# Graph layer in one kernel: edge features in one transfer, 512-column products, and another order where layers meet

## The chip, the cores and the metric

The kernel runs on one core of a Trainium2 chip. The metric is the device time in microseconds (us) of one launch. TensorE multiplies and transposes, VectorE (DVE in the profile) and ScalarE (ACT) do elementwise work, GpSimd (POOL) issues the gathers, and SyncE (SP) issues nearly all other transfers.

## The reference

A graph with 3125 nodes of 256 features and 100,000 edges sorted by destination, all in float32. Cut to what matters:

```python
xn = layernorm(x)
# graph part: one message per edge, summed per destination
m   = concat([xn[src], edge_attr_3])                  # 256 + 3 features
h_N = segment_sum(relu(m @ W1.T + b1), dst)
gnn = l2_normalize(relu(concat([xn, h_N]) @ W2.T))
# mixer part: four layers over all nodes
h = xn
for l in range(4):
    a = layernorm(h)
    q = softmax over each head's 32 features of (a @ Wq) * scale
    k = softmax over all nodes of (a @ Wk) * scale
    h = h + (q @ (k.T @ v)) @ Wo + bo                 # v = a @ Wv
    h = h + gelu(layernorm(h) @ W1 + b1) @ W2 + b2
x = x + gnn + h
# sixteen experts, two per node, with weights from a gate
return x + layernorm(y + moe(y)),  y = layernorm(x)
```

## The kernel before, in words

Nodes stand as 25 tiles of 125, grouped in seven blocks: five of four tiles, one of three and one of two. The activations stay in on-chip memory (`xm`). The mixer is written as stages over one block: `stage_k` and `stage_q` (products with Wk, Wq and their softmax steps), `stage_ek` and `stage_qT` (transposes of the results), `stage_m` (the running sum of k and a), `context` (L508: from the finished sum to one matrix `mo`, a chain of four short products with VectorE or ScalarE between them), `stage_y`, `stage_ln2`, `stage_t2`, `stage_f1`, `stage_f2` (the feed-forward part), and `stage_stats`, `stage_ln1`, `stage_t1` (layer norm for the next layer). The order of calls from L655 to L734 is written out by hand and is the order of TensorE, ScalarE and GpSimd; VectorE and SyncE are put in order by the framework's scheduler, at build time.

The edge part runs beside the layers. By linearity, `xn @ W1h` is computed once (`stage_proj`) and stored in memory. Edges are cut into 784 chunks of 128, eight chunks to a group, 98 groups. For each chunk GpSimd gathers 128 rows (L255, `load_chunk`). A group is split in four strips of two chunks; a strip has one of four row groups of TensorE.

- `message_step` (L284): the product of the three edge features (and a one, for the bias) with their weights, `pw` (L294), one product of 256 columns for each chunk; VectorE adds it to the gathered rows (L298), ScalarE applies relu (L299), VectorE makes the one-hot matrix `hot` (L301).
- `sum_step` (L265): products with `hot` sum a group's messages into 32 destinations per strip (`pq`, L279); the sum of two groups ago is transposed (`win_ps`, L270) and added to `hNT` (L273).

A planner spreads these steps. Each has a due place in groups (`due`, L308): gathers 1.25 groups ahead, messages at half, sums at whole numbers. Each stage reports its TensorE columns by `worked`, which advances `place` and runs the steps that have come due; so they enter the order between two stages' instructions. A gather that comes due waits for a one-element copy (`tick`, L334) of the stage's result, so that GpSimd isn't ahead of the stage. The calls `worked(12 * D)` stand where TensorE would have nothing else; in the last layer, `stage_g` (products of the graph update) takes these places.

What is left of the plan is flushed at L730. Then all engines read a flag (L802) and take or skip a branch (`any_order`, for inputs whose destinations lie far apart; skipped here). The memory of the edge phase is then given to the pool `gates`.

Of the kernel before, what the change touches and what calls it, by code (L numbers as in the profile page):

```python
# [17 lines left out]
D = 256  # L18
P = 128
# [45 lines left out]
def gps_layer(ctx: ExitStack, tc: tile.TileContext, a, out):  # L65
# [60 lines left out]
    with ExitStack() as ph:  # L126
# [9 lines left out]
        def mm_tile(name):  # L136
            return psum.tile([P, 512], F32, tag="mm", name=name)
# [37 lines left out]
        w1w = edge.tile([P, D], F32, name="w1w", bufs=1)  # L175
# [25 lines left out]
        for s in range(S):  # L201
            nc.sync.dma_start(w1w[s * W:s * W + 4, :], a["gnn_W1w"])
# [40 lines left out]
        def load_chunk(c):  # L243

            g, j = divmod(c, G)
            if j == 0:
                ea = edge.tile([P, SC * P], F32, name="ea")
                for s in range(S):
                    e0 = (g * S + s) * SC * P
                    nc.sync.dma_start(ea[s * W:s * W + 4, :], a["eaT"][:, e0:e0 + SC * P])  # L250
                groups_[g] = [], ea
            gats = groups_[g][0]
            if j % (G // 2) == 0:
                gats.append(edge.tile([P, 2, SC, D], F32, name="gat", bufs=6))
            nc.gpsimd.indirect_dma_start(  # L255
                out=gats[-1][:, (j // SC) % 2, j % SC, :], out_offset=None, in_=proj,
                in_offset=bass.IndirectOffsetOnAxis(ap=src_i[:, c:c + 1], axis=0))
# [26 lines left out]
        def message_step(g):  # L284
            if g % 2 == 0:
                bases.extend(nc.values_load_multi_w_load_instructions(
                    base_i[:, g * S:min((g + 2) * S, NS)], engines=[mybir.EngineType.DVE],
                    min_val=0, max_val=N - 1,
                    skip_runtime_bounds_check_because="a dst is a node")[1])
            gats, ea = groups_[g]  # L290
            pws = [mm_tile("pw").rearrange("p (i d) -> p i d", i=SC) for _ in range(S)]
            for i in range(SC):
                for s in range(S):
                    nc.tensor.matmul(pws[s][:, i, :], ea[s * W:s * W + 4, i * P:(i + 1) * P],  # L294
                                     w1w[s * W:s * W + 4, :], start=True, stop=True)
            for s in range(S):
                msg = gats[s // 2][:, s % 2]
                nc.vector.tensor_add(msg, msg, pws[s])  # L298
                nc.scalar.activation(msg, msg, AF.Relu)  # L299
# [105 lines left out]
        def stage_stats(b):  # L405
            for t in BLOCKS[b]:
                stats(tmp, xm[:, t, :], t)
# [100 lines left out]
        def context(l):  # L508
# [8 lines left out]
            worked(12 * D)  # L517
# [6 lines left out]
            worked(12 * D)  # L524
# [128 lines left out]
        with tc.manual_schedule(engines=in_order):  # L653

            prepared = windows()  # L655
            stage_xn(0)
            stage_xh1(0)
            stage_xnT(0)
# [3 lines left out]
            for b in range(NB + 1):  # L662
                if b < NB:
                    stage_k(0, b)
                    if b + 2 < NB:
                        stage_xn(b + 2)
                    stage_q(0, b)
                if b > 1:
                    next(prepared, None)
                if b > 0:  # L670
                    stage_m(0, b - 1)
                if b + 1 < NB:
                    stage_xh1(b + 1)
                    stage_xnT(b + 1)
# [4 lines left out]
                if b < NB:  # L679
                    if b > 1:  # L680
                        next(prepared, None)
                    stage_ek(0, b)
                    stage_qT(0, b)
                if b == NB - 2:
                    for _ in prepared:
                        pass
                    spread = True
            for l in range(last):
                start_layer(l)
                context(l)  # L690
                load(l + 1, "Wk", "Wq", "Wv")
                stage_y(l, 0)
                stage_ln2(0)
                stage_y(l, 1)
                worked(12 * D)
                stage_t2(l, 0)
                worked(12 * D)
                for b in range(NB):
# [13 lines left out]
                    stage_stats(b)  # L712
                    if b > 0:
                        stage_k(l + 1, b - 1)
# [4 lines left out]
                    stage_ln1(b)  # L719
                stage_ek(l + 1, NB - 2)  # L720
                stage_qT(l + 1, NB - 2)
# [11 lines left out]
            stage_qT(last, NB - 1)  # L733
            stage_m(last, NB - 1)  # L734

        def any_order():
# [13 lines left out]
            def chunk(e0, n):  # L750
# [33 lines left out]
                nc.tensor.matmul(pw[:n, 0, :], ea[:4, :n], w1w[:4], start=True, stop=True)  # L784
# [26 lines left out]
        w2n = wts.tile([P, KC, D], F32, tag="wq", name="w2n")  # L811
# [120 lines left out]
        with tc.manual_schedule(engines=in_order - {mybir.EngineType.Pool}):  # L932
# [3 lines left out]
            parts = [(0, slice(0, 1)), (0, slice(1, 2)), (1, slice(0, 1))]  # L936

            def worked(columns, mark=None):
                if columns == 12 * D and parts:
                    stage_g(*parts.pop(0))  # L940

            context(last)
            stage_y(last, 0)
            stage_ln2(0)
# [267 lines left out]
def device_arrays(inputs):  # L1212
# [16 lines left out]
    d = {"x": i["x"], "eaT": np.pad(eaT, ((0, 0), (0, fill))), "src": i["src"], "dst": i["dst"]}  # L1229
    d["src_c"], d["dst_c"] = chunked(i["src"]), chunked(i["dst"])  # L1230
    w1 = i["L0_gnn_W1"]
    d["gnn_W1h"], d["gnn_W1w"] = w1[:, :D].T, np.concatenate([w1[:, D:].T, i["L0_gnn_b1"][None]])
# [33 lines left out]
```

## Time and profile before

| | us |
|---|---|
| median of 3 runs (1987.17 to 1989.06) | 1988.45 |
| the profiled execution's own time | 1994.73 |
| its span, first to last instruction | 1993.0 |
| TensorE busy | 1807.7 |
| VectorE, ScalarE, GpSimd busy | 1165.1, 743.6, 1126.5 |
| gathers, L255, 784 of them | 761.9 |
| `pw`, L294, 1568 records (two passes for each product) | 114.6 |

How to read it: a matmul of float32 shows as two records, one for each pass; a transpose shows as one. The busy time of a group of matmuls is the union of its records, since they overlap. The granted clock (PEclk) is the share of TensorE's full speed that it was given. The layers' boundaries lie at about 135, 530, 950 and 1350 us; the experts run from about 1690 to 1918 us.

### The profile page before, as it was taken

Reading aid. Unit: us, or ns where it says so; the run is one execution under the profiler, and the core shown is the slowest. Engines: PE = TensorE matmul, PEld = TensorE weight load, DVE = VectorE, ACT = ScalarE, POOL = GpSimd, SP = SyncE. Lnnn points to the kernel's source line nnn. Section 1 sums busy time; section 2 is a strip of 40 time slices with the busy share of each in tenths; the row PEclk is TensorE's granted clock in tenths of the full one; section 3 lists DMA queues with packets and bytes.
Section 4 is the critical chain, followed back from the end, with each engine's and each line's share of the span. In section 5 each row is a group of like instructions: output and inputs, shape, how many; then the busy total and the mean of one; then the engine's idle time right before and its main releaser. Section 6 shows DMA issues by size and latency. Waiting matters only on the chain. (4 is left out here: it accounts for less than half of the span.)

```text
span 1993.0 us, 30766 instructions
## 1 busy us (share of the span) xinstructions
PE 1807.7 (91%) x9749; PEld 1269.3 (64%) x9749; DVE 1165.1 (58%) x3761; ACT 743.6 (37%) x1343; POOL 1126.5 (57%) x1429
## 2 busy tenths in 40 slices
PE   6988999999888999999889999998999994999963
PEld 4764656666655666667546666666777783888841
DVE  7654566666664666766656666765646653333326
ACT  3543444344533444544333444443222231222202
POOL 1026777677667777777677777771114435545512
PEclk9998999999988999999889999999999996999987
DMA  6123333233433233334423233333211113777744
GB/s 188 66 77 92 89 85 88 79 88 93 129 98 91 84 93 91 89 84 127 118 81 89 85 90 87 89 89 100 67 29 29 28 19 116 241 259 260 273 130 120
DMA packets 83294, 210.74 MB, mean 106 GB/s; under 512 B 26523, under 2 KB 42306, under 8 KB 78389
## 3 DMA queue, kind: packets, MB, share of 16 engines
q0 software_dynamic: 44800, 118.16, 20.6%
q1 hardware_dynamic: 37246, 87.31, 13.9%
q10 hardware_dynamic: 1078, 3.20, 0.6%
q8 instruction: 84, 1.38, 0.3%
q14 instruction: 86, 0.70, 0.1%
HBM read 187.34 MB, written 21.19 MB: 105 GB/s over the span
## 5 line engine op out<-in xcount | busy, mean ns | idle before, releaser
L255 POOL DMA_INDIRECT gat<-proj,src_i x784 | 761.9, 972 | 212.4 <-issue 163.4
L581 PE MATMUL f_ps<-h2T,ww 128*128 128x500 f32 (+2 forms) x896 | 360.6, 551 | 6.4 <-ACT h2T L339 5.8
L299 ACT ACTIVATE gat<-gat 128x512 f32<-128x512 f32 x392 | 237.6, 630 | 341.0 <-DVE gat L298 315.4
L591 PE MATMUL f_ps<-ww,gT 128*125 128x256 f32 x1600 | 362.3, 382 | 0.0
L298 DVE TENSOR_TENSOR gat<-gat,pw 128x512 f32<-128x512 f32 x392 | 245.5, 680 | 162.1 <-PE pw L294 138.3
L591 PEld LDWEIGHTS f_ps<-ww,gT 128*125 128x125 f32 x1600 | 295.1, 188 | 58.4 <-issue 10.5
L581 PEld LDWEIGHTS f_ps<-h2T,ww 128*128 128x128 f32 x896 | 167.0, 192 | 168.5 <-issue 122.8
L583 ACT ACTIVATE gT<-f_ps,ffb 128x500 f32<-128x500 f32 (+2 forms) x224 | 135.6, 631 | 136.4 <-PE f_ps L581 135.8
L279 PE MATMUL pq<-gat,hot 128*32 128x256 f32 x1568 | 137.6, 405 | 22.4 <-ACT gat L299 22.3
L273 DVE TENSOR_TENSOR hNT<-hNT,win_ps 128x64 f32 x392 | 84.7, 216 | 74.4 <-PE win_ps L270 64.4
L925 POOL DMA_INDIRECT slots<-rec,at x50 | 59.5, 1189 | 110.0 <-DVE rs_u L113 63.7
L596 DVE TENSOR_TENSOR xm<-xm,f_ps 125x512 f32<-125x512 f32 (+1 forms) x52 | 34.7, 667 | 138.7 <-PE f_ps L591 136.4
L1120 PE MATMUL e_ps<-ew,hs 128*128 128x256 f32 x464 | 112.8, 381 | 2.2 <-DVE o L1124 2.2
L294 PE MATMUL pw<-w1w,ea 4*128 4x256 f32 x1568 | 114.6, 403 | 0.0
L1127 POOL DMA_INDIRECT outs<-o,ids x58 | 57.4, 989 | 100.6 <-DVE o L1125 97.5
L458 PE MATMUL q_ps<-wwq,hT 128*125 128x256 f32 x400 | 99.8, 402 | 4.6 <-DVE gat L298 3.6
L563 POOL TENSOR_TENSOR xm<-xm,b 125x1024 f32<-125x1024 f32 (+2 forms) x28 | 59.9, 2140 | 77.6 <-DVE xh L122 58.5
L547 PE MATMUL y_ps<-mo,qT 128*125 128x256 f32 x400 | 98.0, 397 | 4.9 <-DVE mo L538 4.9
L294 PEld LDWEIGHTS pw<-w1w,ea 4*128 4x128 f32 x1568 | 72.5, 185 | 45.0 <-issue 34.5
L495 PE MATMUL m_ps<-xh,ek 125*128 125x257 f32 x400 | 97.9, 398 | 1.8 <-ACT ek L481 1.8
L279 PEld LDWEIGHTS pq<-gat,hot 128*32 128x32 f32 x1568 | 49.6, 112 | 77.9 <-ACT gat L299 45.3
L1120 PEld LDWEIGHTS e_ps<-ew,hs 128*128 128x128 f32 x464 | 85.2, 190 | 20.4 <-issue 4.5
(222 smaller groups left out, 2652.8 us busy)
## 6 DMA issues: line engine op xcount, KB each, us to landing
ew<-ffn_w SPq DMA_DIRECT2D x37, 1154.0 KB
gat<-proj,src_i POOLq DMA_INDIRECT x784
ww<-mix_W SPq DMA_DIRECT2D x8, 1024.0 KB
ea<-eaT SPq DMA_DIRECT2D x392, 4.0 KB
ogs<-outs SPq DMA_DIRECT2D x6, 448.0 KB
ogs<-outs ACTq DMA_DIRECT2D x6, 448.0 KB
out<-ogs SPq DMA_DIRECT2D x6, 448.0 KB
xnT_d<-stage SPq DMA_DIRECT2D x5, 500.0 KB
```

Source lines behind the costliest of these rows:

```text
L255: nc.gpsimd.indirect_dma_start(out=gats[-1][:, (j // SC) % 2, j % SC, :], out_offset=None, in_=proj, in_offset=bass.IndirectOffsetOnAxis(a ...
L279: nc.tensor.matmul(pq[s * W:(s + 1) * W, :], hot[:, s * SC + i, :], gats[s // 2][:, s % 2, i, :], start=(i == 0), stop=(i == SC - 1))
L294: nc.tensor.matmul(pws[s][:, i, :], ea[s * W:s * W + 4, i * P:(i + 1) * P], w1w[s * W:s * W + 4, :], start=True, stop=True)
L298: nc.vector.tensor_add(msg, msg, pws[s])
L299: nc.scalar.activation(msg, msg, AF.Relu)
L458: nc.tensor.matmul(ps[:, i, :], hT[:, c, cols(o + i)], wt["Wq"][:, c, :], start=(c == 0), stop=(c == KC - 1))
L495: nc.tensor.matmul(ps, st["ek", b][:, i, c * P:(c + 1) * P], xh1s[b % 2][:, i, :], start=(i == 0), stop=(i == n - 1))
L547: nc.tensor.matmul(ps[:, i, :], qT[:, c, cols(t0 + i)], mo[:, c, :], start=(c == 0), stop=(c == KC - 1))
L581: nc.tensor.matmul(ps, wt["W1"][:, c, f * P:(f + 1) * P], st["h2T", b][:, c, :m], start=(c == 0), stop=(c == KC - 1))
L583: nc.scalar.activation(gT[:, f, :m], ps, AF.Gelu, bias=ffb[:, l, f:f + 1])
L591: nc.tensor.matmul(ps[:, i, :], st["gT", b][:, f, cols(o + i)], wt["W2"][:, f, :], start=(f == 0), stop=(f == NF - 1))
L1120: nc.tensor.matmul(ps[:, j, :], x["hs"][:, f, j * P:(j + 1) * P], x["w2"][:, f, :], start=(f == 0), stop=(f == NEF - 1))
```

## The change

- Edge features: they are laid out on the host as one block of 128 x 128 numbers for each group, each strip's two chunks in eight rows, the rest zero. One transfer for a group takes the place of four.
- Products: the weights are laid out as eight rows of 512 columns, block-diagonal, so that one product of eight rows gives both chunks of a strip side by side. There are four products for a group instead of eight.
- Start: `stage_xnT` goes ahead of `stage_xh1`.
- Changes of layer: the planner is held (`held`) from the last block's statistics to `stage_y` of block 0 of the next layer; at fixed places in between, `fill(2)` runs up to one message and `fill(1)` up to one sum, with the gathers that stand ahead of them and no `tick`. The last block's layer norm goes ahead of `stage_k` of the block before. The last block's `stage_q` moves into `context`, its `stage_qT` behind `stage_y` of block 1. The columns of the held part are taken out of `total`, which makes the plan's rate higher elsewhere.
- End: in the last layer's `context` the places are taken by `stage_q` and three parts of `stage_g`; `w2n` no longer takes the place of Wq, which is still in use, and lies in `gates`.

```diff
-                ea = edge.tile([P, SC * P], F32, name="ea")
-                for s in range(S):
-                    e0 = (g * S + s) * SC * P
-                    nc.sync.dma_start(ea[s * W:s * W + 4, :], a["eaT"][:, e0:e0 + SC * P])
+                ea = edge.tile([P, P], F32, name="ea")
+                nc.sync.dma_start(ea, a["ea_g"][g])
...
-            pws = [mm_tile("pw").rearrange("p (i d) -> p i d", i=SC) for _ in range(S)]
-            for i in range(SC):
-                for s in range(S):
-                    nc.tensor.matmul(pws[s][:, i, :], ea[s * W:s * W + 4, i * P:(i + 1) * P],
-                                     w1w[s * W:s * W + 4, :], start=True, stop=True)
+            pws = [mm_tile("pw") for _ in range(S)]
+            for s in range(S):
+                nc.tensor.matmul(pws[s], ea[s * W:s * W + SC * 4, :], w1w[s * W:s * W + SC * 4, :],
+                                 start=True, stop=True)
+            pws = [pw.rearrange("p (i d) -> p i d", i=SC) for pw in pws]
...
-        total = (DEPTH - 1) * (attention + forward + 60 * D)
+        at_end = sum(len(r) * (2 * KC * TP + KC * D + 2 * KC * P + KC * (D + 1)) for r in BLOCKS[-2:])
+        total = (DEPTH - 1) * (attention + forward) - (DEPTH - 1) * (at_end + BT * KC * D)
...
-            if not spread:
+            if not spread or held:
                 return
...
+        def fill(kind):
+
+            while due and due[-1][1] in (0, kind):
+                _, k, step, i = due.pop()
+                step(i)
+                if k == kind:
+                    return
...
-            worked(12 * D)
+            between[0]()
             ps = mm_tile("meanT_ps").rearrange("p (h m) -> p h m", h=KC)
...
-            worked(12 * D)
+            between[1]()
             ps = mm_tile("ctx_ps")[:, :D].rearrange("p (c m) -> p c m", c=KC)
...
-            worked(12 * D)
+            between[2]()
             ps = mm_tile("mo_ps").rearrange("p (c d) -> p c d", c=KC)
...
+            between[3]()
...
+            stage_xnT(0)
             stage_xh1(0)
-            stage_xnT(0)
...
-                context(l)
+                more = (lambda kind: None) if l == 0 else fill
+                context(l, [lambda: stage_q(l, NB - 1), lambda: more(1), lambda: None, lambda: more(2)])
                 load(l + 1, "Wk", "Wq", "Wv")
                 stage_y(l, 0)
+                held = False
                 stage_ln2(0)
                 stage_y(l, 1)
-                worked(12 * D)
+                stage_qT(l, NB - 1)
                 stage_t2(l, 0)
-                worked(12 * D)
...
                     stage_stats(b)
+                    if b == NB - 1:
+                        stage_ln1(b)
+                        held = True
+                        fill(2)
                     if b > 0:
                         stage_k(l + 1, b - 1)
...
                 stage_ek(l + 1, NB - 2)
-                stage_qT(l + 1, NB - 2)
                 stage_t1(l + 1, NB - 1)
                 stage_m(l + 1, NB - 2)
                 stage_k(l + 1, NB - 1)
-                stage_q(l + 1, NB - 1)
+                stage_qT(l + 1, NB - 2)
                 stage_ek(l + 1, NB - 1)
-                if l + 1 < last:
-                    stage_qT(l + 1, NB - 1)
-                    stage_m(l + 1, NB - 1)
+                fill(1)
+                stage_m(l + 1, NB - 1)
...
-        w2n = wts.tile([P, KC, D], F32, tag="wq", name="w2n")
+        w2n = gates.tile([P, KC, D], F32, name="w2n")
...
-            parts = [(0, slice(0, 1)), (0, slice(1, 2)), (1, slice(0, 1))]
...
-            context(last)
+            context(last, [lambda: stage_q(last, NB - 1), lambda: stage_g(0, slice(0, 1)),
+                           lambda: stage_g(0, slice(1, 2)), lambda: stage_g(1, slice(0, 1))])
             stage_y(last, 0)
+            stage_qT(last, NB - 1)
```

More of the change, by code (lines that the diff above doesn't have):

```diff
@@ L174, in gps_layer @@
         w1h = wts.tile([P, KC, D], F32, tag="wo", name="w1h")
-        w1w = edge.tile([P, D], F32, name="w1w", bufs=1)
+        w1w = edge.tile([P, SC * D], F32, name="w1w", bufs=1)
         proj = dram.tile([N, D], F32, name="proj")
@@ L201, in gps_layer @@
         for s in range(S):
-            nc.sync.dma_start(w1w[s * W:s * W + 4, :], a["gnn_W1w"])
+            nc.sync.dma_start(w1w[s * W:s * W + SC * 4, :], a["gnn_W1w"])
         nc.sync.dma_start(ffb, a["mix_b1"])
@@ L503, in stage_m, with context @@
             worked(n * KC * (D + 1), msum[:1, 0, :1])
-        def context(l):
+        def context(l, between):
             nonlocal mo
@@ L661, in gps_layer @@
             stage_t1(0, 0)
[L662 to L666, printed above, removed]
+            for b in range(NB):
+                stage_k(0, b)
+                if b + 2 < NB:
+                    stage_xn(b + 2)
+                if b < NB - 1:
                     stage_q(0, b)
+                else:
+                    held = True
                 if b > 1:
@@ L672, in gps_layer @@
                 if b + 1 < NB:
+                    stage_xnT(b + 1)
                     stage_xh1(b + 1)
-                    stage_xnT(b + 1)
                     if b > 1:
@@ L678, in gps_layer @@
                     stage_t1(0, b + 1)
[L679 to L682, printed above, removed]
+                if b > 1:
+                    next(prepared, None)
+                stage_ek(0, b)
+                if b < NB - 1:
                     stage_qT(0, b)
@@ L687, in gps_layer @@
                     spread = True
+            stage_m(0, NB - 1)
             for l in range(last):
                 start_layer(l)
-                context(l)
+                more = (lambda kind: None) if l == 0 else fill
+                context(l, [lambda: stage_q(l, NB - 1), lambda: more(1), lambda: None, lambda: more(2)])
                 load(l + 1, "Wk", "Wq", "Wv")
                 stage_y(l, 0)
+                held = False
                 stage_ln2(0)
                 stage_y(l, 1)
-                worked(12 * D)
+                stage_qT(l, NB - 1)
                 stage_t2(l, 0)
-                worked(12 * D)
                 for b in range(NB):
@@ L712, in gps_layer @@
                     stage_stats(b)
+                    if b == NB - 1:
+                        stage_ln1(b)
+                        held = True
+                        fill(2)
                     if b > 0:
@@ L718, in gps_layer @@
                         stage_q(l + 1, b - 1)
-                    stage_ln1(b)
+                    if b < NB - 1:
+                        stage_ln1(b)
                 stage_ek(l + 1, NB - 2)
-                stage_qT(l + 1, NB - 2)
                 stage_t1(l + 1, NB - 1)
@@ L732, in gps_layer @@
                 step(i)
-            stage_qT(last, NB - 1)
-            stage_m(last, NB - 1)
         def any_order():
@@ L783, in chunk @@
                 pw = mm_tile("pw").rearrange("p (i d) -> p i d", i=2)
-                nc.tensor.matmul(pw[:n, 0, :], ea[:4, :n], w1w[:4], start=True, stop=True)
+                nc.tensor.matmul(pw[:n, 0, :], ea[:4, :n], w1w[:4, :D], start=True, stop=True)
                 nc.vector.tensor_add(gat[:n, 0, :], gat[:n, 0, :], pw[:n, 0, :])
@@ L935, in gps_layer @@
             load_update(1)
-            parts = [(0, slice(0, 1)), (0, slice(1, 2)), (1, slice(0, 1))]
             def worked(columns, mark=None):
-                if columns == 12 * D and parts:
-                    stage_g(*parts.pop(0))
-            context(last)
+                pass
+            context(last, [lambda: stage_q(last, NB - 1), lambda: stage_g(0, slice(0, 1)),
+                           lambda: stage_g(0, slice(1, 2)), lambda: stage_g(1, slice(0, 1))])
             stage_y(last, 0)
+            stage_qT(last, NB - 1)
             stage_ln2(0)
@@ L1229, in device_arrays @@
     d = {"x": i["x"], "eaT": np.pad(eaT, ((0, 0), (0, fill))), "src": i["src"], "dst": i["dst"]}
+    ea = np.moveaxis(d["eaT"].reshape(4, NG, S, SC, P), 0, 3).reshape(NG, S, SC * 4, P)
+    d["ea_g"] = np.pad(ea, ((0, 0), (0, 0), (0, W - SC * 4), (0, 0))).reshape(NG, P, P)
     d["src_c"], d["dst_c"] = chunked(i["src"]), chunked(i["dst"])
     w1 = i["L0_gnn_W1"]
-    d["gnn_W1h"], d["gnn_W1w"] = w1[:, :D].T, np.concatenate([w1[:, D:].T, i["L0_gnn_b1"][None]])
+    w1w = np.concatenate([w1[:, D:].T, i["L0_gnn_b1"][None]])
+    d["gnn_W1h"] = w1[:, :D].T
+    d["gnn_W1w"] = np.concatenate([np.pad(w1w, ((0, 0), (j * D, (SC - 1 - j) * D))) for j in range(SC)])
     d["gnn_W2"] = i["L0_gnn_W2"].T
```

## The prediction

> **What bounds the kernel now.** I read the page first (busy shares, then the slices), then a table of windows by stage, then PE's waits, the timeline of one change of layer, and last GpSimd's rows in a steady stage.
>
> ```profile
> PE 1807.7 (91%) x9749; PEld 1269.3 (64%) x9749; DVE 1165.1 (58%) x3761; ACT 743.6 (37%) x1343; POOL 1126.5 (57%) x1429
> PEclk9998999999988999999889999999999996999987
> ```
>
> TensorE is busy for 91% of the span, so time can come only from less TensorE work, from its gaps, or from the clock in the stages where slices fall to 8. The windows show which stages these are:
>
> ```profile
> core 0: us, PE busy (x) PEld busy (x) DVE busy (x) ACT busy (x) POOL busy (x), PEclk, DMA share, GB/s
> 120.00:195.00 75.00, 60.13 (x310) 38.07 (x308) 38.63 (x120) 26.73 (x51) 43.61 (x57) 0.86 0.33 96
> 195.00:529.00 334.00, 323.45 (x1932) 217.36 (x1931) 209.27 (x623) 148.48 (x261) 244.37 (x340) 0.98 0.32 91
> 529.00:613.00 84.00, 67.52 (x397) 40.96 (x396) 54.24 (x170) 31.57 (x58) 55.00 (x74) 0.88 0.37 108
> 950.00:1022.00 72.00, 56.53 (x317) 34.12 (x315) 45.54 (x139) 26.20 (x49) 47.11 (x60) 0.83 0.33 94
> 1022.00:1345.00 323.00, 315.00 (x1871) 209.22 (x1863) 206.73 (x609) 145.47 (x254) 238.43 (x334) 0.98 0.31 88
> 1345.00:1415.00 70.00, 58.02 (x310) 47.94 (x306) 38.41 (x134) 19.63 (x39) 7.81 (x20) 0.95 0.33 96
> ```
>
> Inside a layer only 3% is idle, at clock 0.98. The four changes of layer lose more. Idle plus (1 - clock) x window: 14.9 + 10.5 = 25.4 us, 16.5 + 10.1 = 26.6, 15.5 + 12.2 = 27.7, 12.0 + 3.5 = 15.5. Together 95 us: what the new order works on. What ends the gaps:
>
> ```profile
> PE qT_ps L144 <- DVE qs L469: 24.6, 8, 4.9
> PE pq L279 <- ACT gat L299: 22.3, 16, 3.9
> PE h2T_ps L144 <- DVE xh L122: 7.7, 4, 3.5
> ```
>
> The first is the last block's softmax, whose transposes stand right behind it; the second is a sum placed too soon after its message. One change of layer (start, length, gap in brackets):
>
> ```profile
> 530.32 2.79 PE L432 MATMUL k_ps<-hT,wwk 128*128 128x375 f32 x8
> 533.04 1.15 PE L294 MATMUL pw<-w1w,ea 4*128 4x256 f32 x16
> 534.12 2.86 PE L458 MATMUL q_ps<-wwq,hT 128*125 128x256 f32 x12
> 542.57 0.82 PE L144 MATMUL qT_ps<-ident,qs 125*128 125x125 f32 x4 [4.89 <-DVE qs L469]
> ```
>
> GpSimd looks free at 57%, but these rows of 195 to 529 us and a piece of timeline say otherwise:
>
> ```profile
> L255 POOL DMA_INDIRECT gat<-proj,src_i x216 | 210.7, 975 | 57.4 <-issue 45.2 <-ACT gT L583 2.6 <-PE f_ps L581 1.0
> L563 POOL TENSOR_TENSOR xm<-xm,b 125x1024 f32<-125x1024 f32 (+2 forms) x6 | 12.5, 2082 | 10.4 <-DVE xh L122 10.3
> 704.66 0.97 POOL L255 DMA_INDIRECT gat<-proj,src_i  x1 [0.16 <-issue]
> 705.93 0.95 POOL L255 DMA_INDIRECT gat<-proj,src_i  x1 [0.30 <-issue]
> ```
>
> A gather holds the queue for 1.27 us (705.93 - 704.66), 1.31 with a tick between. In this window 216 x 1.29 + 12.5 = 291 of 334 us: 87% taken.
>
> **Part 1, products of 512 columns.** The trace's single records of a message step (L294) start four at a time, within 0.02 us, at 0, 0.32, 0.54 and 0.75 us; the next matmul starts at 1.08, in nearly every group. A round of 256 columns thus takes 0.216; the first is 0.10 longer, because the second pass's weights (0.18 us, begun 0.11 after the first product) arrive late, and leaving costs 0.11. After: two rounds of 0.43, which hide those weights, and 0.11: 0.97. Saved 0.105 x 98 = 10.3 us, at worst none. If the four no longer ran beside each other it would be 8 x 0.43 = 3.4 us a group; since the row groups stay the same I exclude that but for a rest. Rule: the Trainium skill, "TensorEngine Tiling (Array Packing)", section Instruction Overhead, gives each matmul some 60 cycles. At the trace's 256 columns in 0.216 us that is 0.05 us, and 8 instructions fewer in 98 groups would save 40 us (an estimate). The starts 0.02 apart show it hidden: I take 10.3.
>
> **Part 2, one transfer.** The SP queue issues 98 instead of 392 (0.295 us each, 114 us in all); SP is issuing for 343 us of 1993, so nothing follows. A transfer now has 128 rows of 512 B instead of 16 of 1 KB; at a DMA share of 0.32 and a lead of over a group (11 us) it is hidden. Cost 0; if it came late, the wait would stand at L294.
>
> **Part 3, start.** In layer 0 the copy of xnT goes ahead of four ACT activations of 0.43 us. TensorE waits 6.9 us for that copy in seven places; about 3 us go. hT waits for these activations later, behind 3 to 5 us of proj.
>
> **Part 4, changes of layer.** From f2 of the last block to the next f1, six groups of edge work stand now (529 to 596); two stay, the last block's q becomes the filler of the context, its qT goes behind y. I added up the new order, in the middle of the run, with t = 0 at the end of f2. TensorE: sum and message 2.4, k(5) and q(5) 5.6, so ek(5) could start at 8.0. VectorE: xm 0.7, stats 1.1, window adds and mask 1.4, layer norm of block 6 about 2.8 (11 small operations of 0.16 to 0.2, two of 0.4), four message adds of 0.63, two k reductions of 0.42 to 0.55, kmax/alpha/neg 0.5; then two exps on ACT of 0.48: ek(5) starts at about 12.3. The message adds now stand ahead of the k reductions: gap 4.2, about what the old qT gap was. Further: m(5) behind ACT's exps 0.7; ek(6) behind k(6) and exp 1.2; ctx behind q(6)'s softmax, which stands ahead of meanT's affine on VectorE (0.69 x 2, exp 0.63, 0.69, 0.54), 2.9; mo 0.7; then y is 7.4 us of TensorE, while VectorE has four message adds 2.5, four pairs of xm and stats at 1.7, eighteen rsqrt steps 2.6 and two normalizations 0.7, so h2T waits 4.4; f1 1.2. Idle 15.3 (16.5 now). For the clock I put 6 us: three gaps, a half-speed stretch each of 3.4 to 6.8 us, half lost. 21.3 against 26.6 and 27.7: gains 5 and 6. First change, with no message in it: 10.7 idle + 6 against 25.4: gain 9. Last: qT gaps (3.4 + 3.3) go, a k wait of 2.8 comes, the update products cover mo and ctx; w2n moves to memory that the edge phase frees, so its 256 KB is issued on SP after the branch at 1391, not at 1383.6; first use about 3 us later. I put 1.5 us (none to 3). 9.6 against 15.5: gain 6. Sum 26; bounds 0 (all gaps return elsewhere) and 60 (two thirds of 95).
> Rule: the Trainium skill, "TensorE: Matmul & The Clock Gate", section Why this matters for your kernels, halves the clock only after gaps over about 3 us. That speaks against holding the filler back, but by it just the 4.2 and 4.4 would count, 3.4 us. Here 574.4 to 580.4 ran at 0.50 behind gaps of at most 2.1 us, so I keep 6.
>
> **Part 5, the rate between.** What is held must fit elsewhere: the plan's total falls from 729,330 to 646,536 columns, so groups come 12.8% denser, every 11.0 us instead of 12.4 (334 us for 216/8 groups). VectorE rises from 63 to 66% and is not the bound. GpSimd in the first layer: 265 gathers x 1.29 + 7 x 2.4 = 359 us, against some 357 us of TensorE (345 by rows, 12 of gaps); second 344 against 352; third 332 against 357. Waits for the xm add (10.3 in the old window) and ticks come on top unless GpSimd lags. Gathers now end some 3 us ahead of their message, and a late one stops VectorE with all behind it: k, softmax, affine. Against that, sums stand better: fewer follow within 4.3 us of their message, its shortest latency (22.3 us of PE waits now, mostly counted in part 4). I put +8, from 0 to +60.
>
> **Sum** against the profiled run's 1994.7 us (span 1993.0): -10.3 - 3 - 26 + 8 = -31, giving 1963. The median of the runs is 6.3 lower, so 1957. A measurement of this kernel can tell about 0.2%, 4 us, from no change.
>
> **Rivals.**
> - GpSimd becomes the bound (slower). If the old window's waits stay (xm 10.3, ticks 22, so 32 a layer), the layers overshoot by 34, 24 and 7 us: 65 us against 39 saved, 1988 + 26 = 2014. It turns from gain to loss at some 21 us of waits a layer. For: the 1.27 us period, the ten-microsecond xm wait at 254. Against: a lagging queue finds its marks ready, and 13 gathers are issued ahead at each change. Half the waits give 1970 to 1985.
> - The gaps truly close: VectorE, free of four groups of message work (4 us each), ends its chains sooner; half of the boundaries' remaining 69 us go too: about 1925. Against: the order still puts message adds ahead of the k reductions.
> - The gaps only move: Part 4 gives nothing, Part 1 stays: 1980 to 1985.
>
> **Numbers.** Forecast 0.55 (1940 to 1974). GpSimd 0.22, half of it slower. Gaps close 0.10. Gaps only move 0.13, a little of it within 0.2% or beyond. Faster 0.85, same 0.04, slower 0.11. Range 1930 to 1988.
>
> **What would show it.** Right: L294's step 0.97 us, its PE busy near 100; clock at the changes above 0.88; no qT wait on qs; new waits ek on ekT, ctx on meanT, h2T on xh. Wrong: VectorE waiting for gat transfers by tens of us, GpSimd gathers back to back through the layers, and TensorE gaps inside 195 to 529.

## The result, and the profile after

| | before | after |
|---|---|---|
| median of 5 runs, us | 1988.45 (1986.76 to 1989.06) | 1970.48 (1962.86 to 1974.01) |
| ratio to before, 95% interval | 1 | 0.9907 (0.9883 to 0.9931) |
| profiled execution, its span, us | 1994.73, 1993.0 | 1972.88, 1971.2 |

The kernel is 0.9% faster, 18 us by the medians and 22 us by the profiled executions. The forecast was 1957 in a range of 1930 to 1988: the sign was right, the gain was about 60% of the one forecast (18 of 31 us). The page's rows of TensorE and of the granted clock, after:

```profile
PE 1808.7 (92%) x8965; PEld 1227.4 (62%) x8965; DVE 1167.1 (59%) x3761; ACT 744.8 (38%) x1343; POOL 1122.7 (57%) x1404
PEclk8999999999989999999889999999999996999987
```

784 records fewer (98 groups x 8), and TensorE is busy for 1.0 us *longer*. So the change took nothing off TensorE's work. The 22 us come out of its gaps and of the clock. The table of windows, cut at the stages of the kernel after, shows where:

```profile
core 0: us, PE busy (x) PEld busy (x) DVE busy (x) ACT busy (x) POOL busy (x), PEclk, DMA share, GB/s
120.00:180.00 60.00, 50.08 (x199) 32.51 (x198) 29.21 (x97) 18.93 (x36) 18.24 (x26) 0.89 0.21 62
180.00:527.00 347.00, 338.10 (x1847) 211.81 (x1846) 224.80 (x667) 160.65 (x281) 282.63 (x385) 1.00 0.37 107
527.00:585.00 58.00, 47.59 (x181) 30.90 (x180) 36.52 (x115) 19.05 (x34) 14.71 (x17) 0.82 0.22 64
...
937.00:995.00 58.00, 47.02 (x192) 30.35 (x191) 36.63 (x119) 17.90 (x33) 15.88 (x18) 0.82 0.22 66
995.00:1329.00 334.00, 327.58 (x1779) 201.68 (x1778) 217.73 (x647) 157.70 (x276) 265.42 (x357) 0.99 0.36 101
1329.00:1395.00 66.00, 55.60 (x261) 46.21 (x260) 34.51 (x135) 16.11 (x33) 5.11 (x11) 0.92 0.29 92
```

By the prediction's own measure, idle plus (1 - clock) x window, the four changes of layer lose 9.9 + 6.6 = 16.5, 10.4 + 10.4 = 20.8, 11.0 + 10.4 = 21.4 and 10.4 + 5.3 = 15.7 us. Before it was 25.4, 26.6, 27.7 and 15.5. The first three gained 9, 6 and 6, the last nothing.

A finer account takes each record of the clock. What is lost is the time in which TensorE is idle, plus half of the busy time at half clock; what remains is work at full speed (all in us).

| stage | lost before | lost after | difference |
|---|---|---|---|
| start, 0 to 120 us | 22.8 | 23.7 | +0.9 |
| first change | 22.7 | 15.8 | -6.9 |
| first layer | 15.7 | 10.5 | -5.2 |
| second change | 26.3 | 19.8 | -6.5 |
| second layer | 8.0 | 6.8 | -1.2 |
| third change | 25.6 | 20.6 | -4.9 |
| third layer | 13.1 | 8.6 | -4.6 |
| last change | 14.9 | 14.8 | -0.2 |
| graph update and experts | 89.8 | 89.1 | -0.7 |
| (not lost) work at full speed, whole kernel | 1754.2 | 1761.6 | +7.5 |

The sum is -21.8, the difference of the two profiled executions. Of the 7.5 us of added work, 6.5 lie in the message products, which were meant to get shorter: `pw` is busy for 122.2 us instead of 114.6, and less half of its time at half clock for 120.1 instead of 113.6. TensorE's waits after:

```profile
engine line waited for: us in total, times, longest us
...
PE h2T_ps L144 <- DVE xh L122: 12.9, 4, 3.9
...
PE pq L278 <- ACT gat L298: 9.1, 12, 2.6
PE m_ps L504 <- ACT ek L490: 6.4, 5, 2.5
...
PE ek_ps L489 <- ACT ekT L456: 6.0, 5, 2.0
PE ctx_ps L537 <- ACT meanT L348: 5.5, 3, 2.2
PE k_ps L441 <- DVE hT L350: 5.2, 1, 5.2
PE proj_ps L408 <- ACT stage L398: 3.7, 5, 2.3
```

The wait of qT for the softmax (24.6 us) is gone, and that of the sums for their messages fell from 22.3 to 9.1. In their place stand ek on ekT, ctx on meanT, more of m on ek, and a longer h2T on xh: the chains that the filler used to cover.

### The profile page after: what moved, and what is told of

It is laid out like the page before. It is cut to its first block, busy times and chain, and to the rows that moved or that the text cites. A ratio compares the mean times of both kernels' runs of the same rounds, so it can differ in the third digit from the quotient of the medians.

```text
span 1971.2 us, 28535 instructions
## 1 busy us (share of the span) xinstructions
PE 1808.7 (92%) x8965; PEld 1227.4 (62%) x8965; DVE 1167.1 (59%) x3761; ACT 744.8 (38%) x1343; POOL 1122.7 (57%) x1404
## 3 DMA queue, kind: packets, MB, share of 16 engines
q0 software_dynamic: 44800, 118.16, 20.8%
q1 hardware_dynamic: 48254, 92.17, 14.9%
## 5 line engine op out<-in xcount | busy, mean ns | idle before, releaser
L591 PE MATMUL f_ps<-h2T,ww 128*128 128x500 f32 (+2 forms) x896 | 367.0, 558 | 7.8 <-ACT h2T L348 6.2
L297 DVE TENSOR_TENSOR gat<-gat,pw 128x512 f32<-128x512 f32 x392 | 250.6, 677 | 174.5 <-PE pw L292 158.0
L278 PE MATMUL pq<-gat,hot 128*32 128x256 f32 x1568 | 123.7, 386 | 9.7 <-ACT gat L298 9.1
L292 PE MATMUL pw<-w1w,ea 8*128 8x512 f32 x784 | 122.2, 649 | 0.6 <-DVE qs L474 0.4
L441 PE MATMUL k_ps<-hT,wwk 128*128 128x500 f32 (+2 forms) x224 | 92.9, 558 | 5.9 <-DVE hT L350 5.2
L1135 PEld LDWEIGHTS e_ps<-ew,hs 128*128 128x128 f32 x464 | 85.2, 190 | 20.4 <-issue 4.5
L557 PEld LDWEIGHTS y_ps<-mo,qT 128*125 128x125 f32 x400 | 78.1, 200 | 24.6 <-issue 7.2
```

The source lines that it names most:

```text
L278: nc.tensor.matmul(pq[s * W:(s + 1) * W, :], hot[:, s * SC + i, :], gats[s // 2][:, s % 2, i, :], start=(i == 0), stop=(i == SC - 1))
L292: nc.tensor.matmul(pws[s], ea[s * W:s * W + SC * 4, :], w1w[s * W:s * W + SC * 4, :], start=True, stop=True)
L557: nc.tensor.matmul(ps[:, i, :], qT[:, c, cols(t0 + i)], mo[:, c, :], start=(c == 0), stop=(c == KC - 1))
L591: nc.tensor.matmul(ps, wt["W1"][:, c, f * P:(f + 1) * P], st["h2T", b][:, c, :m], start=(c == 0), stop=(c == KC - 1))
L1135: nc.tensor.matmul(ps[:, j, :], x["hs"][:, f, j * P:(j + 1) * P], x["w2"][:, f, :], start=(f == 0), stop=(f == NEF - 1))
```

## The experiments

The ratios are against the kernel before on the same chip. Its median was 1991.39 us on the chip of products and transfer alone, of the two runs on the order, and of the one without the hold; 2224.29 us on the chip of the four variants of the hold (a slower one); and 1990.55 us on the chip of the other four.

### Products and transfer alone

The kernel before with its old order, and only the edits of the edge features:

```diff
-                for s in range(S):
-                    nc.sync.dma_start(ea[s * W:s * W + 4, :], a["eaT"][:, e0:e0 + SC * P])
+                nc.sync.dma_start(ea, a["ea_g"][g])
...
-            for i in range(SC):
-                for s in range(S):
-                    nc.tensor.matmul(pws[s][:, i, :], ...)          # 8 products of 256 columns
+            for s in range(S):
+                nc.tensor.matmul(pws[s], ...)                        # 4 products of 512 columns
```

> The kernel before, with one transfer a group and products of 512 columns, and no other order. Theory A (entering and leaving the row-group mode costs about 0.10 us each, whatever the number of columns): a message step takes 1.07 us from its first product to the next matmul as before, and the time stays within 3 us of 1988. Theory B (the prediction: late weights of the second pass, hidden behind 512 columns): 0.97 us a step, about 10 us faster, 1978. Theory C (products that hold four banks until the last of two long rounds make TensorE wait inside the step): steps of over 1.1 us become more frequent, 5 to 8 us slower.

Measured: 1981.0 us, 0.9948 (0.9928 to 0.9969). About 10 us, the size that the prediction gave for the products. But the message step did not get shorter, as the next run shows. The gain has another source.

### What a message step is made of

The changed kernel with its four products issued twice over:

```diff
-            for s in range(S):
+            for s in [*range(S), *range(S)]:
                 nc.tensor.matmul(pws[s], ea[s * W:s * W + SC * 4, :], w1w[s * W:s * W + SC * 4, :],
```

> The changed kernel with the four products of 512 columns of each message step issued twice over, so that a step streams four rounds instead of two and its result is the same. It measures what a step is made of. If a step pays once for going into the row groups and once for coming out (0.105 us each, the reading of 0.535 for the first round and 0.536 for the second), the starts of the rounds stand at 0, 0.535, 0.97 and 1.40 us and the next matmul at 1.93 us. If each round carries its own 0.105 us of late weights (the reading behind the prediction, applied to every round), the rounds are 0.535 apart and the step takes 2.14 us. If the second four ran beside the first, it would stay near 1.07. One look; 98 steps x 0.86 us = 84 us more TensorE work, so a time near 2055 us.

One message step and what follows, in the timeline of the changed kernel, and then of this one (start, length):

```profile
644.14 1.14 PE L292 MATMUL pw<-w1w,ea 8*128 8x512 f32 x8
645.21 3.72 PE L601 MATMUL f_ps<-ww,gT 128*125 128x256 f32 x16
```

```profile
651.27 2.00 PE L292 MATMUL pw<-w1w,ea 8*128 8x512 f32 x16
653.20 5.30 PE L591 MATMUL f_ps<-h2T,ww 128*128 128x500 f32 x12
```

From the step's start to the next matmul: 1.07 and 1.93 us. The single records of this kernel start, four at a time, at 0, 0.534, 0.963 and 1.392 us, and the next matmul at 1.93. The inner rounds take 0.429; only the first and the last are longer, by 0.105 and 0.109. That is the first reading to the hundredth: a fixed 0.21 us a step, half at its start and half at its end, whatever is done between. The weights are not it: in the changed kernel those of the second pass are loaded by 0.29 us, and its round starts at 0.53 all the same. That it is the price of going into the row groups and of coming out is a reading: between groups of ordinary products less stands (L627 and L630 in the last change: 0.87 and 0.93 us for four rounds of 0.216). Two rounds of 0.43 stream the same columns as four of 0.216, so the step goes from 1.076 to 1.071 us: 0.5 us in 98 steps, not 10.3. The whole kernel took 2062.62 us in its one run, where near 2055 was expected.

### The transfer alone

The kernel before with the one transfer, and eight products of 256 columns over the eight rows:

```diff
-                    nc.tensor.matmul(pws[s][:, i, :], ea[s * W:s * W + 4, i * P:(i + 1) * P],
-                                     w1w[s * W:s * W + 4, :], start=True, stop=True)
+                    nc.tensor.matmul(pws[s][:, i, :], ea[s * W:s * W + SC * 4, :],
+                                     w1w[s * W:s * W + SC * 4, i * D:(i + 1) * D], start=True, stop=True)
```

> The kernel before with the one transfer and the wider weights, but eight products of 256 columns as it had them, in its old order. Products plus transfer gave 0.9948 of the kernel before, although a message step is no shorter in the trace. If the gain came with the transfer (294 fewer issues on SP, the features there sooner), this kernel keeps it: 0.994 to 0.997. If it came with the products of 512 columns (fewer instructions, or sums that wait less behind a differently shaped step), this one stands at 1.000 within 0.002. If one long transfer is dearer than four short ones, it is above 1.002.

Measured: 1989.1 us, 0.9997 (0.9983 to 1.0012). The transfer is worth nothing that can be told, so the 0.9948 belongs to the products. Where does it come from, if their step is no shorter? TensorE's waits, without and then with products of 512 columns:

```profile
PE pq L277 <- ACT gat L300: 21.4, 15, 4.2
...
PE h2T_ps L144 <- DVE gat L299: 7.2, 4, 2.0
```

```profile
PE pq L277 <- ACT gat L297: 18.5, 16, 4.7
...
PE h2T_ps L144 <- DVE gat L296: 1.9, 6, 0.8
```

Both wait less for messages. Read one message step in the two VectorE timelines: it starts at 446.57 us in the first kernel, at 439.82 in the second, at the same place of the order.

```profile
447.94 1.48 DVE L122 TENSOR_SCALAR xh<-xm,mv,rstd 125x256 f32<-125x256 f32 x4
449.34 2.47 DVE L299 TENSOR_TENSOR gat<-gat,pw 128x512 f32<-128x512 f32 x4
```

```profile
440.98 0.69 DVE L296 TENSOR_TENSOR gat<-gat,pw 128x512 f32<-128x512 f32 x1
...
441.73 0.41 DVE L122 TENSOR_SCALAR xh<-xm,mv,rstd 125x256 f32<-125x256 f32 x1
442.05 1.28 DVE L296 TENSOR_TENSOR gat<-gat,pw 128x512 f32<-128x512 f32 x2
```

In the first, the four message adds stand behind the whole normalization, 2.77 us after the step's start; in the second the first add comes after 1.16 us and the others between the normalizations. The transposes behind it, which wait for the adds, wait 1.78 us in the first and 0.18 in the second, where the products of q wait another 0.62. VectorE's order is made by the framework's scheduler, and with other products it made another order. All of VectorE's 3761 instructions stand in the same order in the kernel before and in the one with the transfer alone. With the wide products some 190 are moved, and some 80 of them are message adds. Where VectorE was free both start the adds after 1.16 us; on average over 98 steps the first add comes after 1.77 us and 1.36 us. Between the two profiled executions (1988.5 and 1977.2 us) TensorE is idle for 5.7 us less, loses 2.2 us less at half clock, and has 3.4 us less of work at full speed. This is read from the two traces. No run fixed VectorE's order and changed the products alone, so this cause is argued and not shown by experiment.

### The order alone, and the order with the transfer

The changed kernel with the old transfers and products (the first experiment's edit turned round), and the changed kernel with the new transfer but eight products of 256 columns:

```diff
-            for s in range(S):
-                nc.tensor.matmul(pws[s], ...)                        # 4 products of 512 columns
+            for i in range(SC):
+                for s in range(S):
+                    nc.tensor.matmul(pws[s][:, i, :], ...)          # 8 products of 256 columns
```

> The changed kernel with the old transfers and products (four transfers, eight products of 256 columns a group); the new order stays. Theory A: about the changed kernel's time, 1968 to 1972. Theory B: 10 us slower than the changed kernel, about 1981. Theory C: 5 to 8 us faster than the changed kernel, about 1964.

> The changed kernel with one transfer a group, but eight products of 256 columns over the same eight rows. It parts the transfer from the width of the products. If the transfer (128 rows of 512 B, 64 KB) costs something by contention with the gathers, this lies with the changed kernel and above the one with the old transfers too; if only the width matters, it lies with the latter. Expected: no difference by the transfer, under 3 us.

Measured: the order alone 1975.96 us, 0.9921 (0.9904 to 0.9938); with the transfer 1974.24 us, 0.9914 (0.9893 to 0.9935). So the order is worth 16 us (0.79% of 1991) where the prediction had 3 + 26 - 8 = 21. Adding the products to it leads to 0.9907: no gain that can be told from none. The parts do not add. In the old order the sums waited 21.4 us for messages, which earlier adds could shorten. In the new order, without the wide products, they wait 6.4:

```profile
PE pq L278 <- ACT gat L301: 6.4, 10, 1.3
PE h2T_ps L144 <- DVE gat L300: 5.8, 4, 1.7
```

The wide products bring the second of these to 1.8, but the first to 9.1, and the message products stand for 4 us longer (116.3 to 120.1 at full speed).

### Without the hold

The changed order of stages, but messages and sums spread as before, also through the changes of layer:

```diff
-        total = (DEPTH - 1) * (attention + forward) - (DEPTH - 1) * (at_end + BT * KC * D)
+        total = (DEPTH - 1) * (attention + forward)
...
-            if not spread or held:
+            if not spread:
...
-                more = (lambda kind: None) if l == 0 else fill
+                more = lambda kind: None
...
-                        held = True
-                        fill(2)
...
-                fill(1)
```

> The changed kernel without the hold: the planner runs on through the changes of layer (fill is not called, the total counts all columns again), in the new order of stages. Theory H (the hold is what pays: messages at a change of layer stand in VectorE's queue ahead of the chain that TensorE waits for): most of the gain goes, 1982 to 1990. Theory O (the order of stages pays, q as a filler in the context and qT behind y): most of the gain stays, 1968 to 1976. GpSimd's waits for ticks inside the layers should come back to some 20 us a layer, as its rate falls by 12%.

Measured: 1966.92 us, 0.9878 (0.9858 to 0.9899), a little below what theory O expected. The hold is not what brings the gain; which of the other moves does was not tested one by one. In the trace TensorE is idle for 4 us more than in the changed kernel (166.4 and 162.4), but loses 4 us less at half clock (42.9 and 47.1), and the message products stand for 116.0 instead of 120.1. GpSimd's waits for ticks came back in part: 12, 9 and 18 us in the three layers, against 21, 21 and 25 before and 1, 7 and 7 in the changed kernel.

### A slower chip: four variants of the hold

Four kernels ran together: the changed kernel as it is; the one without the hold, with `stage_y(last, 1)` also ahead of `stage_t2(last, 0)`; a short hold, only from the start of `context` to the y of block 0; and gathers half a group earlier.

```diff
             stage_y(last, 0)
...
-            stage_t2(last, 0)
             stage_y(last, 1)
+            stage_t2(last, 0)
```

```diff
-        at_end = sum(len(r) * (2 * KC * TP + KC * D + 2 * KC * P + KC * (D + 1)) for r in BLOCKS[-2:])
+        at_end = len(BLOCKS[-1]) * KC * D
...
                 start_layer(l)
+                held = True
...
-                        held = True
-                        fill(2)
...
-                fill(1)
```

```diff
-        LEAD = 1.25
+        LEAD = 1.75
```

> The changed kernel once more, beside the next three on one chip, since its runs spread over 11 us and the differences are of that size. Expected: 1963 to 1974, ratio about 0.991 to the kernel before.

> The kernel without the hold, and in the last layer y of block 1 ahead of the transposes of block 0, where TensorE waited 3.5 us for xh in the changed kernel and without the hold. If the run without the hold was truly faster, it stays 5 us or more below the changed kernel on this chip; the second edit should take 3 us of wait (h2T on xh) and the half-speed stretch behind it, 3 to 5 us more: about 1960 to 1964. If the hold made no difference: 1966 to 1970.

> As the last one, but the planner is held from the start of the context to y of block 0, with fill at its places there; it runs on through the products behind the last block. If it is the hold at the end of a layer that costs (a message ahead of the k reductions), this is as fast as without any hold, 1960 to 1964. If the hold in the context costs as well (no filler for ctx and h2T, so the half-speed stretches stay), it lies between that and the changed kernel.

> The changed kernel with gathers due 1.75 instead of 1.25 groups ahead. If GpSimd is merely late (lead too short), VectorE's waits for gathers (15 us) and the sums' waits go down and the time falls by 3 to 8 us. If GpSimd is at its rate in the first layer, a longer lead moves nothing, within 3 us of the changed kernel, since it starts no earlier than the layer.

| kernel | us | ratio |
|---|---|---|
| changed kernel | 2230.07 | 1.0020 (1.0001 to 1.0038) |
| no hold, y swapped | 2175.18 | 0.9776 (0.9752 to 0.9800) |
| short hold, y swapped | 2187.38 | 0.9828 (0.9802 to 0.9854) |
| gathers earlier | 2226.24 | 1.0008 (0.9986 to 1.0030) |

Every kernel is 11 to 13% slower on this chip than on the others, and the changed kernel's gain is gone, while the version without the hold keeps more than its own. The short hold lies between the two, as the second branch of its expectation had it; it differs from the version without the hold in the hold alone, so 0.5% is the hold's in `context`. What the swap of y does here was not separated. With earlier gathers VectorE's waits for them fell from 20.6 to 3.4 us, but the time fell by no more than the runs spread, so late gathers are not what costs here. The waits of ScalarE and of VectorE of the changed kernel on this chip show something that they do not show on the others:

```profile
ACT osb L281 <- remote: 170.3, 21, 14.1
```

```profile
DVE hot L300 <- remote: 82.9, 20, 9.4
```

"Remote" means that the view saw the signal that released the instruction, but found no instruction whose end it was. ScalarE's copy of a sum and VectorE's next `hot` both wait for the end of a sum. The copy comes over 3 us behind the sum's last recorded product 43 times here, against 7 times for the same kernel on an ordinary chip, and in 33 of the 43 a `hot` starts within 0.1 us of it: in one case 308.76 and 308.70 us, where that product ended at 301.9. What holds the end of a sum back is open, and so is why the hold suffers more from it. No trace of the kernel before was kept on this chip, and all its runs were taken together, so that the chip and the moment are not told apart.

### The best candidate beside the changed kernel

The version of 0.9776, and the changed kernel once more, on an ordinary chip:

> The changed kernel without hold and fill, and with the second y of the last layer ahead of the first transposition behind it: the kernel that stood at 0.9776 on another chip, where the changed kernel stood at 1.002. If what the hold costs is a matter of the order alone, this is faster here too: 0.9878 of the version without the swap, less up to 3 us for the swap, so 0.986 to 0.988, 1962 to 1966 us. If the swap gains nothing, 0.9878. If most of the gap on the other chip was that chip's own stalls, the gap to the changed kernel shrinks here from 2.4% to 0.3 to 0.5%.

> The changed kernel unchanged, on the chip of the other three, so that they are compared on one chip. 0.9907 of the kernel before where it was first timed, 1.002 on another chip. If the first number is the kernel's and the second that chip's, 0.989 to 0.993 here.

Measured: without the hold 1970.62 us, 0.9906 (0.9889 to 0.9922); changed kernel 1970.36 us, 0.9899 (0.9878 to 0.9921). They can't be told apart, and the first misses its expectation of 0.986 to 0.988. The changed kernel's gain shows again, and the 2.4% between the two were seen on the slower chip alone. The swap moved a wait: h2T waits 1.0 us for xh where it waited 3.5, but f1 behind it then waits 4.8 us for VectorE's h2T. With 0.9878 in its own comparison, the version without the hold and without the swap had the lowest ratio of all, but its interval (to 0.9899) reaches into that of the changed kernel. No version was found that beats it for certain.

## Why the prediction was right, and where it was wrong

The sign was right, and so was the mechanism for the first three changes of layer. The time came near the forecast in part by luck: the products, the start, the rate and the last change each went wrong, in both directions. Two of the prediction's own signs failed: the step at L294 takes 1.07 us and not 0.97, with 122 us busy instead of 100, and the clock at two of the changes is 0.82, not above 0.88. The others came: no wait of qT, and new waits of ek, ctx and h2T.

**Products (forecast -10.3; measured -10 alone, about -1 with the new order).** The failed step is "the second pass's weights arrive late". The 0.10 us at the first round is a fixed price of the step, which wider products do not hide: 1.071 us a step, not 0.97. The 10 us of the first experiment came, by the two traces, by way of VectorE's order, and agree with the forecast by chance. The price of some 60 cycles for each instruction (the Trainium skill, "TensorEngine Tiling (Array Packing)", section Instruction Overhead), from which the prediction estimated 40 us and which it set aside, is not seen here either: half the instructions, and 0.005 us less a step.

**Transfer (0).** Right: 0.9997.

**Start (-3; measured +1).** TensorE's wait for the copies fell from 6.9 to 3.7 us, the 3 us of the forecast, and k of block 0 starts 2.9 us sooner (17.56 instead of 20.44). But k's wait for hT rose from 2.5 to 5.2. The failed step is that only the ScalarE activations were counted for hT. They were in time: hT's transposes end at 16.8 us, ScalarE's half of hT at 17.5. VectorE's half stands in its order behind the statistics of the next blocks and a reduction over all destinations (`least`), and starts at nearly the same time before and after:

```profile
22.11 0.96 DVE L213 TENSOR_REDUCE least<-drel 128x392 f32<-128x784 f32 x1
22.99 0.97 DVE L341 TENSOR_SCALAR hT<-hT_ps,lnp 128x250 f32<-128x250 f32 x2
```

```profile
22.85 0.97 DVE L350 TENSOR_SCALAR hT<-hT_ps,lnp 128x250 f32<-128x250 f32 x2
```

So the idle time of this stage fell by 0.4 us only, and the loss at half clock rose by 1.3.

**Changes of layer (-9, -5, -6, -6).** The first three were right in sum: -20 was forecast, -21 measured by the same reckoning, -18.3 by the finer one. Their split between gaps and clock was not. One change in the timeline of the kernel after:

```profile
528.42 2.75 PE L467 MATMUL q_ps<-wwq,hT 128*125 128x256 f32 x12
533.21 1.28 PE L489 MATMUL ek_ps<-ident,ekT 128*125 128x128 f32 x6 [2.03 <-ACT ekT L456]
...
535.62 4.30 PE L504 MATMUL m_ps<-xh,ek 125*128 125x257 f32 x12 [0.70 <-ACT ek L490]
...
543.14 0.95 PE L489 MATMUL ek_ps<-ident,ekT 128*125 128x128 f32 x4 [0.90 <-ACT ekT L456]
...
551.60 0.49 PE L537 MATMUL ctx_ps<-meanT,wwv 128*128 128x128 f32 x2 [2.19 <-ACT meanT L348]
...
558.51 9.09 PE L557 MATMUL y_ps<-mo,qT 128*125 128x256 f32 x32
...
570.75 1.41 PE L144 MATMUL h2T_ps<-ident,xh 125*128 125x125 f32 x8 [2.72 <-DVE xh L122]
572.82 2.04 PE L591 MATMUL f_ps<-h2T,ww 128*128 128x500 f32 x2 [0.65 <-ACT h2T L348]
```

Each gap that was forecast is there, in its place: ek 4.2 us forecast and 2.0 seen, m 0.7 and 0.7, the second ek 1.2 and 0.9, ctx 2.9 and 2.2, h2T 4.4 and 2.7, f1 1.2 and 0.65. The idle time is 10.4 us, not 15.3, and the clock took 10.4 us, not 6. Three things made the difference. First, the terms that Part 4 lists add up to 10.0 us for VectorE's chain for ek (to `neg`) and to 11.0 for ek, not to the 12.3 that it went on with. Second, `neg` ended 9.2 us after the end of f2, because the small steps of the layer norm stand between the message adds, each starting just before the one ahead ends, and ek started behind the first of ScalarE's two exps, at 9.8. Third, h2T's input came 12.2 us after the start of y, close to the 7.4 + 4.4 = 11.8 forecast (the terms listed for it add up to 12.6); but y ran at half clock for part of it and took 9.1 us instead of 7.4, so that some of what was booked as a gap became a slow product.

The mis-sized term is the clock's. Its records show three half-speed stretches, the number forecast, at 535.1 to 538.5, 552.2 to 562.4 and 572.7 to 579.5 us: 20.4 us together, where the forecast's 6 us are half of 12. A rule of no idle gaps over about 3 us (the Trainium skill, "TensorE: Matmul & The Clock Gate", section Why this matters for your kernels), read as a limit, would have given full speed: no gap in this window is over 2.72 us. The forecast set it aside, and rightly, but then put less for the clock than the trace of before had shown at the changes (10.1 to 12.2 us).

**Last change (-6; measured -0.2).** This is the largest error in this part. The qT gaps went, as forecast (3.4 + 3.3), and among others these gaps stand there now:

```profile
1335.63 1.05 PE L278 MATMUL pq<-gat,hot 128*32 128x256 f32 x10 [2.64 <-ACT gat L298]
...
1351.84 0.78 PE L144 MATMUL hT_ps<-ident,xh 125*128 125x125 f32 x4 [1.47 <-DVE xh L122]
...
1358.45 0.95 PE L489 MATMUL ek_ps<-ident,ekT 128*125 128x128 f32 x4 [0.90 <-ACT ekT L456]
...
1391.91 1.95 PE L144 MATMUL h2T_ps<-ident,xh 125*128 125x125 f32 x8 [3.48 <-DVE xh L122]
```

The k wait of 2.8 came as 1.5, at hT. The update products do cover ctx and mo, as said, and no wait for `w2n`, put at 1.5 us, appears. But each product that moves brings its VectorE work along. VectorE's timeline behind the first y, before and then after, with one of the rows of the update's own norm (`sq`):

```profile
1408.40 0.75 DVE L90 BATCH_NORM_STATS2 bnst<-xm 125x6 f32<-125x256 f32 x2
...
1413.52 1.38 DVE L122 TENSOR_SCALAR xh<-xm,mv,rstd 125x256 f32<-125x256 f32 x4
```

```profile
1383.44 0.75 DVE L90 BATCH_NORM_STATS2 bnst<-xm 125x6 f32<-125x256 f32 x2
...
1385.55 0.42 DVE L635 SCALAR_TENSOR_TENSOR sq<-hl 125x256 f32<-125x256 f32 x1
...
1391.35 1.38 DVE L122 TENSOR_SCALAR xh<-xm,mv,rstd 125x256 f32<-125x256 f32 x4
```

From the first statistics to `xh`, for which h2T waits, it takes 7.9 us here and took 5.1 before, when these squares (`sq`) stood ahead of mo and behind `xh`. So h2T waits 3.5 us instead of 1.1. The failed step: the forecast counted the moved products on TensorE and left out what they start on VectorE. It also missed that the last sum before the change now waits 2.6 us for its messages.

**The rate between (+8).** By the finer table the three layers lost 11.0 us less than before, against 7.5 us of added work, so that products and rate together gave -3.5, where -10.3 + 8 = -2.3 was forecast. Two wrong terms nearly cancelled. The rate itself was right by luck: by the kernels' own formulas the plan's totals are 579,330 and 496,536 columns, each 150,000 less than the prediction's, so the groups are due 16.7% denser in columns, not 12.8%. Yet the groups came every 11.0 us, as forecast (347 us for 253/8 groups), since a group's own products (`win_ps`, `pq` and `pw`, about 2.4 us) are not among the plan's columns and do not shrink: 10.0 x 496,536 / 579,330 + 2.4 gives 11.0 (an estimate; 10.0 is the 12.4 of before less 2.4). The fear was GpSimd. Its rows in the first layer after:

```profile
L254 POOL DMA_INDIRECT gat<-proj,src_i x253 | 246.2, 973 | 59.1 <-issue 44.2 <-ACT gT L593 2.5 <-DVE hNT L272 1.7
L573 POOL TENSOR_TENSOR xm<-xm,b 125x1024 f32<-125x1024 f32 (+2 forms) x6 | 12.5, 2087 | 3.8 <-DVE xh L122 3.7
L335 POOL COPY tick<-gT 1x1 f32<-1x1 f32 x49 | 8.7, 178 | 1.2 <-ACT gT L593 1.0
```

Busy 282.6 plus 44.2 of issue is 327 of 347 us: 94% taken, near the edge as worked out. But what would have pushed it over went away. The wait before its xm add is 3.8 us where it was 10.4, and the ticks wait 1 us in this layer where they waited 21, since the marks are ready when they are reached. "A lagging queue finds its marks ready" was the argument against that rival, and it held. VectorE waits for gathers 15.2 us in all, 20.5 before. What the denser groups cost is inside the message step, a term that the forecast did not have. One of them in the timeline:

```profile
314.96 2.52 PE L292 MATMUL pw<-w1w,ea 8*128 8x512 f32 x8
...
317.84 1.96 PE L467 MATMUL q_ps<-wwq,hT 128*125 128x256 f32 x8 [0.37 <-DVE qs L474]
```

It stands between two halves of q and takes 2.9 us to the next matmul instead of 1.07; 14 steps are longer than 1.15 us, 9 before. The kernel with 256 columns in the new order has 12, all among these 14, and the one with 512 columns but without the hold has 7. So the further long steps come with the hold's denser groups, and with wide products they last longer (`pw` at full speed: 113.6 before, 116.3 with 256 columns and the hold, 116.0 with 512 and no hold, 120.1 with both). Time inside a group of matmuls counts as busy, so this cost hides in the busy time and not in the waits.

**The rivals.** GpSimd did not become the bound. The gaps did not close beyond the sum. "The gaps only move" gave 1980 to 1985; it was right for the last change and wrong for the other three.

**Sum.** -31 was forecast, -22 measured in the profiled executions. The difference is the start (4 us), the changes of layer (26 - 18.5 = 7.5, of which the last change 6), and 2 us the other way: products and rate together 1.2, the graph update and the experts 0.7.

## What to carry to other kernels

Two parts of a change that shorten the same wait need not add: cost the second against the waits that the first leaves. Before crediting a shorter step to fewer or wider products, look at single records for a fixed price at the step's start and end, and double the work inside once: it separates the fixed part from the rest in one run. Where a scheduler orders an engine, compare that engine's order in the two kernels too: here, by the traces, an edit on TensorE paid through VectorE's order. When work moves ahead on one engine, follow its input on every engine that makes a part of it: here VectorE's half of hT, and the squares ahead of `xh`, took the gain away. A gain of 1% should be seen on more than one chip, with the rival version beside it.

## What the runs showed of the hardware

- A step of products over four row groups has a fixed price of 0.105 us at its first round and 0.108 at its last, for two and for four rounds, of 256 and of 512 columns (rounds at 0, 0.32, 0.54, 0.75, next matmul 1.076; at 0, 0.534, next 1.071; at 0, 0.534, 0.963, 1.392, next 1.93).
- TensorE's clock averaged 0.82 in a change of layer in which no gap was over 2.72 us, with half-speed stretches of 3.4, 10.2 and 6.8 us.
- One chip ran the kernel before in 2224 us where others took 1988 to 1991. In the changed kernel's trace there the ends of sums reached ScalarE and VectorE several us late, and TensorE was idle for 293 us instead of 162. What causes it was not found; it set two versions 2.4% apart that are equal elsewhere.
